# Exp on VectorE in eight steps with integer bits, in three of four head groups of every block

## The chip, the cores and the metric

The kernel runs on one core of a Trainium2 chip. The metric is the device time of one launch in microseconds. An execution with the hardware profiler gives the trace; times of other executions give the median.

Engines are called as in the profile: PE is TensorE (PEld its weight loads), ACT is ScalarE, DVE is VectorE, POOL is GpSimd, SP is SyncE, which issues most of the DMAs.

## The reference, cut to what matters

Four graph layers run one after the other on a node matrix x (3327 x 128) and an adjacency matrix adj (3327 x 3327). Each is followed by a residual addition and a layer normalisation. Only layer 0 is touched by the change. It is an attention with a transposed view of heads: 128 "heads" d, each with 3327 queries and keys of only 8 features, and adj added twice to the scores.

```python
q = (x @ Wq.T).reshape(d, n, h)          # d = 128, n = 3327, h = 8
k = (x @ Wk.T).reshape(d, n, h)
v = (x @ Wv.T).reshape(d, n, h)
a = jnp.einsum('dnh,dmh->dnm', q, k) * d ** (-0.5)
a = a + adj + adj
a = softmax(a, axis=2)
out = jnp.einsum('dnm,dmh->dnh', a, v).reshape(n, h * d)
return out @ Wo.T
```

So the exponential of 128 x 3327 x 3327 scores has to be taken, about 1.4 billion of them. The later layers multiply adj and its transpose with 128-column matrices.

## The kernel before, in words

**Stages.** The start (to about 319 us in the trace) projects x to queries, keys and values, splits queries and keys in a high and a low half and lays them down in DRAM scratch. The attention (`attention()`, lines 409 to 686) follows, to about 10141 us. The other layers take the rest, to 10914 us.

**Blocks.** The attention goes through 28 blocks: 7 chunks of 476 queries (`CW`), and for each 4 stretches of key tiles of 128 keys (`KBS`, line 80): 7, 7, 6 and 6 tiles. So 14 blocks have seven key tiles and 14 have six. In a block all 128 d are gone through, in 32 groups of four (`GROUP`). A block and a d make one step.

**A step.** Scores of one d are made in three sets of key tiles (`SETS`, line 444): 3, 2 and 2 tiles in a seven-tile block, 2, 2 and 2 in a six-tile block. Each set has its own PSUM buffer `sc` (line 421), one of each, so a set can be refilled only when the exponential of the same set of the step before has been read out. `exponents` (line 594) issues a set's score matmuls (L610) and then its exponential: as a rule one ACT activation (L618), which reads the whole set from PSUM and writes a tile `e` to SBUF with 476 columns per key tile. Only in the first d of a group, and only for the third set (`si` 2), in the groups that `on_vector` (line 446) names, does DVE take the exponential instead: `vector_exp` (line 568). In a seven-tile block these are groups 0, 1 and 2 of every four; in a six-tile block every even group. That is 24 exps in a seven-tile block and 16 in a six-tile block, 560 in all; the other 10192 sets go to ACT.

**Exp on DVE before.** L574 reads the scores from PSUM, clamps them and scales them by 2/ln 2. L575 rounds by adding a large constant, L576 takes the difference of rounded and unrounded value, L577 shifts the rounded number's bits into the exponent and sets mantissa bits, and five steps of L580 evaluate a polynomial; the last of them multiplies by the power of two. Nine instructions on 128 x 952 elements. The tiles `ey` and `et` that they share exist once each.

**Edges.** In the first step of a block (d = 0) adj is first turned into each PSUM buffer by PE transposes (L603), four per key tile; the scores are added onto it. The same PSUM contents serve every later d of the block, because the queries and keys of one d come with the negated ones of the d before: keys and queries have 32 more rows that subtract the previous d's scores. `copy_queries` (line 495) makes these negated copies on DVE, three instructions (L499, L500, L501) per group, one group ahead. `load_edges` (line 429) fetches the edges of the next block with two DMAs on SP's queue, right after the third set of d = 0.

**Weighing.** `weigh` (line 624) multiplies the finished exponentials of one key tile, for the four d of a group, with the values (four matmuls, L635; the trace counts eight). The weighings of a group, 7 or 6, are spread over the next group's twelve places (4 d x 3 sets) by the table `PLACES` (line 452): after the set at place p come as many weighings as the row has entries p. After every third group the sum in PSUM is added to `acc` by DVE (L646, L648).

**What orders the work.** The order on PE, ACT, POOL and DVE in the attention is the program's own (`manual_schedule`). The DVE steps behind the first of an exp, and the query copies, stand in a list `vec`; `vector_work` (line 585) takes from it as long as a running cost of DVE, `clock[1]`, is below that of the sets, `clock[0]` (0.95 per set in seven-tile, 0.84 in six-tile blocks). The first step, L574, is issued at its place. A weighing that needs a DVE exponential takes out of the list what belongs to its group first.

**Background pieces.** In the attention's first 24 blocks or so, the transpose of adj and its row and column sums are made in pieces, one piece in eight groups (`PACE`): load and store in groups 0 of eight, DVE transpose and maximum in group 3, DVE sums in group 7 (`background`, `background_work`, lines 526 and 533).

**Loads.** For every group, SP issues three DMAs of queries (L469) and eight of keys (L476), two groups ahead, and every second group one of values (L511).

Of the kernel before, what the change touches and what calls it, by code (L numbers as in the profile page):

```python
# [19 lines left out]
P = 128  # L20
# [7 lines left out]

POLY = (-7.287735661479654, 41.808648955824374, -180.93753376132258, 522.0867441991364, -753.2122427382569)
ROUND = 1.5 * 2 ** 23 + 127 + 256 - 10
MANTISSA = 3015794
EPS = 1e-5


# [14 lines left out]
def kernel(ctx: ExitStack, tc: tile.TileContext, x, adj, wq, wk, wv, wo,  # L51
# [357 lines left out]
    def attention():  # L409
        with tc.tile_pool(name="acc", bufs=1) as accp, tc.tile_pool(name="kq", bufs=3) as kq, \  # L410
# [15 lines left out]
            groups = [(b, g) for b in range(len(blocks)) for g in range(NHG)]  # L426
            steps = [(b, d) for b in range(len(blocks)) for d in range(D)]

            def load_edges(b):
                c0, kb = blocks[b]  # L430
                k0, nt = KBS[kb]
                w = min(nt * P, N - k0 * P)
                e = ed.tile([P, len(subs), 7 * P], F32, name="e_in")
                if w < nt * P:
                    nc.gpsimd.memset(e[:, :, w:nt * P], 0.0)
                nf = CW // P
# [87 lines left out]
            loaded, worked, turning = [], [], []  # L524

            def background(n):
                if n % PACE == 0 and worked:
                    piece_store(pe, *worked.pop(0))
                if n % PACE == 0 and pieces:
                    u, c = pieces.pop(0)  # L530
                    loaded.append((u, c, piece_load(pe, u, c)))

            def background_work(n):
                if n % PACE == 3 and loaded:
                    u, c, ai = loaded.pop(0)
                    steps = piece_work(pe, u, c, ai)
                    worked.append((u, c, next(steps)))
                    next(steps)
                    clock[1] += 2.4
                    turning.append(steps)  # L540
                if n % PACE == 7 and turning:
                    clock[1] += 2.4
                    for _ in turning.pop():
                        pass

            def prepare(b, d):

# [12 lines left out]

                if d % GROUP == 1 - on_vector(KBS[blocks[b][1]][1], d // GROUP) and n + 1 < len(groups):
# [6 lines left out]
            def vector_exp(e, x, of):  # L568


                y = ex.tile([P, 2, CW], F32, name="ey")
                t = ex.tile([P, 2, CW], F32, name="et")
                ti = t.bitcast(I32)
                nc.vector.tensor_scalar(y, x, -58 * math.log(2.0), 2 / math.log(2.0), ALU.max, ALU.mult)  # L574
                vec.append((0.7, of, lambda: nc.vector.tensor_scalar(t, y, ROUND, None, ALU.add)))  # L575
                vec.append((1.2, of, lambda: nc.vector.scalar_tensor_tensor(y, t, ROUND, y, ALU.subtract, ALU.subtract)))  # L576
                vec.append((0.7, of, lambda: nc.vector.tensor_scalar(ti, ti, 23, MANTISSA, ALU.logical_shift_left,  # L577
                                                                 ALU.bitwise_or)))
# [15 lines left out]
            def exponents(b, d, si):  # L594
# [16 lines left out]
                                     rhs=qt[64 * rg:64 * rg + 64, k, :],  # L611
                                     start=False, stop=True, skip_group_check=True)
                e = ex.tile([P, (3, 2, 2)[si], CW], F32, tag=f"e{si}", name=f"e{si}", bufs=(6, 7, 8)[si])
                if on_vector(nt, d // GROUP) and (d % GROUP, si) == (0, 2):
                    vector_exp(e[:, 0:n, :], s[:, 0:n, 0:CW], (b, d // GROUP))
                    clock[1] += 1.2
                else:
                    nc.scalar.activation(e[:, 0:n, :], s[:, 0:n, 0:CW], AF.Exp, scale=2.0)  # L618
# [42 lines left out]
            queue, place = [], 0  # L661
            with tc.manual_schedule(engines={mybir.EngineType.PE, mybir.EngineType.Activation,
                                             mybir.EngineType.Pool, mybir.EngineType.DVE}):
                edges[0] = load_edges(0)
# [5 lines left out]
                for b, d in steps:  # L670
                    prepare(b, d)
                    for si in range(len(SETS[KBS[blocks[b][1]][1]])):
                        vector_work(b)
                        exponents(b, d, si)
                        for _ in range(PLACES[len(queue_of)][d // GROUP % 4].count(place) if queue else 0):
                            weigh(*queue.pop(0))
                        place += 1
                    if d % GROUP == GROUP - 1:
                        while queue:
                            weigh(*queue.pop(0))  # L680
                        queue_of = [(b, d // GROUP, r) for r in range(KBS[blocks[b][1]][1])]
                        queue, place = list(queue_of), 0
# [562 lines left out]
```

## Time and profile before

| | us |
|---|---|
| median of 3 runs | 10919.42 (10911.48 to 10927.48) |
| the profiled execution's own time | 10915.5 |
| its span, first to last instruction | 10913.7 |
| busy: PE, ACT, DVE, POOL | 10590.0, 9774.0, 8351.7, 1667.9 |
| a block of seven key tiles | 369.75 to 371.5 for most (first 390.75, one 382.5) |
| a block of six key tiles | about 328.75 |

The span is what the engines show; the time adds 1.8 us around it. In the lists of groups a line reads: source line, engine, operation, output <- input with shapes and types, count, then busy us and mean ns of one, then the engine's idle time just before and what ended it. In a timeline a line reads: start, duration, engine, line, operation, how many instructions are merged, and in brackets the idle time of that engine before it and what ended that. In a line of windows each engine's busy time stands with its count of instructions; then follow the granted TensorE clock, the busy share of the DMA engines and GB/s. The granted clock was 0.995 over the run.

### The profile page before, as it was taken

How to read it: one execution, taken by the hardware profiler on the slowest of the kernel's cores; microseconds unless marked ns; L12 is line 12 of the kernel's file. 1: busy time of each engine (PE TensorE's matmuls, PEld its weight loads, DVE VectorE, ACT ScalarE, POOL GpSimd, SP SyncE). 2: the span in 40 equal slices, each digit the busy share in tenths (PEclk: the TensorE clock that was granted, in tenths of full speed). 3: DMA queues.
4: the chain of work that ended last, by engine and by line, in shares of the span. 5: the costliest groups of instructions: out<-in, count | busy, mean ns of one | idle time of the engine just before them, and what ended most of it. 6: DMA issues, size and time to landing. Idle time of an engine off the chain costs nothing. (4 is left out here: it accounts for less than half of the span.)

```text
span 10913.7 us, 202710 instructions
## 1 busy us (share of the span) xinstructions
PE 10590.0 (97%) x76941; PEld 4114.5 (38%) x76941; DVE 8351.7 (77%) x9359; ACT 9774.0 (90%) x10671; POOL 1667.9 (15%) x2742
## 2 busy tenths in 40 slices
PE   8899999999999999999999999999999999999999
PEld 5333333333333333333333333333333333333779
DVE  6788778887788877788877888778887788777312
ACT  3799999999999999999999999999999999999400
POOL 0111122111221111211112111121111100001200
PEclk9899999999999999999999999999999999999999
DMA  7888888888888888888888888888888888788676
GB/s 252 155 127 123 129 133 133 128 124 127 136 133 128 124 127 131 136 123 127 131 131 135 115 122 121 123 133 129 126 129 123 120 119 117 116 111 118 209 283 245
DMA packets 995063, 1516.19 MB, mean 139 GB/s; under 512 B 202471, under 2 KB 812577, under 8 KB 980267
## 3 DMA queue, kind: packets, MB, share of 16 engines
q1 hardware_dynamic: 896854, 1371.75, 77.5%
q0 software_dynamic: 79616, 116.88, 4.7%
q8 instruction: 623, 10.21, 0.5%
q10 hardware_dynamic: 17620, 14.49, 0.4%
q14 instruction: 350, 2.87, 0.1%
HBM read 1371.86 MB, written 130.35 MB: 138 GB/s over the span
## 5 line engine op out<-in xcount | busy, mean ns | idle before, releaser
L618 ACT ACTIVATE e<-sc 128x952 f32<-128x952 f32 (+1 forms) x10192 | 9551.3, 1076 | 281.1 <-PE sc L610 274.7
L635 PE MATMUL o<-e,v_pad 128*32 128x476 f32 (+1 forms) x46592 | 5657.5, 573 | 47.1 <-DVE acc L648 39.8
L610 PE MATMUL sc<-qt,kt 64*128 64x476 f32 x23296 | 4503.2, 439 | 178.4 <-ACT e L618 113.1
L610 PEld LDWEIGHTS sc<-qt,kt 64*128 64x128 f32 x23296 | 2197.0, 184 | 4570.9 <-ACT e L618 4015.0
L580 DVE SCALAR_TENSOR_TENSOR e<-e,ey 128x952 f32<-128x952 f32 x1680 | 1932.7, 1150 | 52.3
L515 POOL COPY v_pad<-vs 128x192 f32<-128x192 f32 (+1 forms) x896 | 534.4, 622 | 7986.1 <-DMA vs<-v_img 5559.1
L635 PEld LDWEIGHTS o<-e,v_pad 128*32 128x32 f32 (+1 forms) x46592 | 1027.9, 108 | 1904.7 <-issue 1858.7
L574 DVE TENSOR_SCALAR ey<-sc 128x952 f32<-128x952 f32 x560 | 643.9, 1150 | 1047.2 <-PE sc L610 1041.2
L501 DVE CAST qt<-qt 64x1904 fp32r<-64x1904 f32 x896 | 1032.8, 1153 | 30.4
L499 DVE TENSOR_SCALAR qt<-qt 32x1428 fp32r<-32x1428 f32 x896 | 807.6, 901 | 159.2 <-DMA qt<-q_s 100.6
L234 POOL DMA_DIRECT2D adjT_s<-at x1352 | 785.3, 587 | 234.5 <-DMA adjT_s<-at 162.2
L580 DVE SCALAR_TENSOR_TENSOR e<-e,et 128x952 f32<-128x952 f32 x560 | 647.5, 1156 | 17.8
L576 DVE SCALAR_TENSOR_TENSOR ey<-et,ey 128x952 f32<-128x952 f32 x560 | 645.1, 1152 | 19.4
L580 DVE SCALAR_TENSOR_TENSOR e<-ey 128x952 f32<-128x952 f32 x560 | 642.0, 1146 | 0.0
L1081 PE MATMUL bank<-y,eT 128*128 128x128 f32 (+1 forms) x4056 | 473.9, 276 | 0.4 <-DVE h L1203 0.4
L1081 PEld LDWEIGHTS bank<-y,eT 128*128 128x128 f32 (+1 forms) x4056 | 465.3, 192 | 5.7 <-DVE h L1203 0.6
L648 DVE TENSOR_TENSOR acc<-o,acc 128x476 f32<-128x476 f32 x231 | 150.3, 651 | 312.4 <-PE o L635 312.0
L575 DVE TENSOR_SCALAR et<-ey 128x952 f32<-128x952 f32 x560 | 372.6, 665 | 18.7
L577 DVE TENSOR_SCALAR et<-et 128x952 int32<-128x952 int32 x560 | 371.1, 663 | 19.3
L500 DVE TENSOR_SCALAR qt<-qt 32x476 fp32r<-32x476 f32 x896 | 360.2, 402 | 7.8 <-DMA qt<-lead_s 3.5
L1041 ACT ACTIVATE rstd<-mv,eps 128x1 f32<-128x1 f32 x104 | 30.4, 293 | 265.5 <-DVE mv L1039 265.5
L655 POOL DMA_DIRECT2D o_s<-acc x308 | 191.4, 625 | 34.9 <-DVE acc L648 22.0
(152 smaller groups left out, 2402.6 us busy)
## 6 DMA issues: line engine op xcount, KB each, us to landing
kt<-k_s SPq DMA_DIRECT2D x5320, 96.0 KB
kt<-k_s SPq DMA_DIRECT2D x1764, 128.0 KB
eT<-adjT_s SPq DMA_DIRECT2D x78, 1664.0 KB
qt<-q_s SPq DMA_DIRECT2D x896, 119.0 KB
qt<-q_s SPq DMA_DIRECT2D x1792, 59.5 KB
vs<-v_img SPq DMA_DIRECT2D x224, 224.0 KB
adjT_s<-at POOLq DMA_DIRECT2D x1352, 32.0 KB, 6.0
vs<-v_img SPq DMA_DIRECT2D x224, 192.0 KB
```

The costliest lines, as they stand in the source:

```text
L234: nc.gpsimd.dma_start(out=flat_ap(adjT_s, (t * P + 32 * q) * NP + c * PIECE, [[NP, 32], [P, ns], [1, P]]), in_=at[32 * i:32 * i + 32].rear ...
L499: return [(0.9, None, lambda: nc.vector.tensor_scalar(qt[32:64, 1:], qf[0:32, 0:GROUP - 1], -1.0, None, ALU.mult)), (0.4, None, lambda: nc ...
L501: (1.2, None, lambda: nc.vector.tensor_copy(qt[64:128], qf[0:64]))]
L515: nc.gpsimd.tensor_copy(vp[:, 32:32 + nt * GROUP * 32].rearrange("p (x c) -> p x c", c=32)[:, :, 0:H], vs.rearrange("p (x c) -> p x c", c=H))
L574: nc.vector.tensor_scalar(y, x, -58 * math.log(2.0), 2 / math.log(2.0), ALU.max, ALU.mult)
L575: vec.append((0.7, of, lambda: nc.vector.tensor_scalar(t, y, ROUND, None, ALU.add)))
L576: vec.append((1.2, of, lambda: nc.vector.scalar_tensor_tensor(y, t, ROUND, y, ALU.subtract, ALU.subtract)))
L580: vec.append((1.2, of, lambda i=i, a=a: nc.vector.scalar_tensor_tensor(e, e if i else y, a, t if i == len(POLY) - 1 else y, ALU.add, ALU.m ...
L610: nc.tensor.matmul(s[:, i, 0:CW], lhsT=kt[64 * rg:64 * rg + 64, k, pos * P:(pos + 1) * P], rhs=qt[64 * rg:64 * rg + 64, k, :], start=False ...
L618: nc.scalar.activation(e[:, 0:n, :], s[:, 0:n, 0:CW], AF.Exp, scale=2.0)
L635: nc.tensor.matmul(o[32 * j:32 * j + 32, 0:CW], lhsT=values[b, g][:m, c:c + 32], rhs=es[b, g * GROUP + j, r][:m, :], start=(r == 0 and u = ...
L1081: nc.tensor.matmul(ps[:n, 0:D], lhsT=e[:m, s, :n], rhs=y[:m, s, col:col + D], start=(s == 0), stop=(s == T - 1))
```

## The change

- **Exp in eight steps.** The first step writes a whole number (int32): the clamped score times 2^24/ln 2. One step takes its upper bits and makes the power of two of them by a bitwise AND and XOR; one takes its lower 23 bits and makes a float between 0.25 and 0.5 of them by AND and OR. Five steps of the polynomial follow, with new coefficients. The step that took the difference (L576) is gone.
- **Which groups.** `on_vector` no longer asks for the kind of block: groups 1, 2 and 3 of every four in all blocks. That is 24 x 28 = 672 exps on DVE and 10080 sets on ACT.
- **Places.** `PLACES` has other rows; the six-tile row is the same for all groups, (0, 2, 4, 6, 8, 10). A new table `FIRST` holds the places in the first group of a block: none before place 4.
- **Edges in four loads.** Each of the four query parts has its own DMA, issued after the third set of d = 0, 8, 16 and 24.
- **Background.** Load and store move to groups 2 of eight, transpose and maximum to groups 4, sums to groups 0.

```diff
-POLY = (-7.287735661479654, 41.808648955824374, -180.93753376132258, 522.0867441991364, -753.2122427382569)
-ROUND = 1.5 * 2 ** 23 + 127 + 256 - 10
-MANTISSA = 3015794
+POLY = (-0.12145248055458069, 1.287218689918518, 0.8447736501693726, 0.7106341123580933, 0.24892811477184296)
+UPPER, LOWER = 0x7F800000, 0x7FFFFF
+EXPONENT, QUARTER = 0x40000000, 0x3E800000
...
-            def load_edges(b):
+            def load_edges(b, j):
...
+                if j == 0:
+                    edges[b] = ed.tile([P, len(subs), 7 * P], F32, name="e_in")
...
-                nc.sync.dma_start(out=e[:, 0:nf, 0:w],
-                                  in_=flat_ap(adj, c0 * N + k0 * P, [[N, P], [P * N, nf], [1, w]]))
-                nc.sync.dma_start(out=e[0:CW - nf * P, nf, 0:w],
-                                  in_=flat_ap(adj, c0 * N + (nf * P * N + k0 * P), [[N, CW - nf * P], [1, w]]))
-                return e
+                q0, n = subs[j]
+                nc.sync.dma_start(out=edges[b][0:n, j, 0:w],
+                                  in_=flat_ap(adj, (c0 + q0) * N + k0 * P, [[N, n], [1, w]]))
...
-            def on_vector(nt, g):
-                return g % 4 != 3 if nt == 7 else g % 2 == 0
+            def on_vector(g):
+                return g % 4 != 0
...
-            PLACES = {7: ((0, 0, 4, 7, 7, 10, 10), (0, 0, 4, 7, 7, 9, 10), (1, 1, 4, 6, 8, 10, 10),
-                          (0, 2, 3, 5, 7, 8, 10)),
-                      6: ((0, 0, 3, 6, 8, 10), (0, 2, 4, 5, 7, 9)) * 2}
+            PLACES = {7: ((0, 2, 4, 4, 7, 7, 9), (0, 0, 3, 7, 7, 10, 10), (0, 0, 3, 6, 6, 9, 9), (0, 0, 3, 6, 7, 10, 10)),
+                      6: ((0, 2, 4, 6, 8, 10),) * 4}
+
+            FIRST = {7: (4, 4, 5, 7, 7, 10, 10), 6: (4, 4, 7, 7, 10, 10)}
...
-                if n % PACE == 0 and worked:
+                if n % PACE == 2 and worked:
...
-                if n % PACE == 0 and pieces:
+                if n % PACE == 2 and pieces:
...
-                if n % PACE == 3 and loaded:
+                if n % PACE == 4 and loaded:
...
-                if n % PACE == 7 and turning:
+                if n % PACE == 0 and turning:
...
-                ti = t.bitcast(I32)
-                nc.vector.tensor_scalar(y, x, -58 * math.log(2.0), 2 / math.log(2.0), ALU.max, ALU.mult)
-                vec.append((0.7, of, lambda: nc.vector.tensor_scalar(t, y, ROUND, None, ALU.add)))
-                vec.append((1.2, of, lambda: nc.vector.scalar_tensor_tensor(y, t, ROUND, y, ALU.subtract, ALU.subtract)))
-                vec.append((0.7, of, lambda: nc.vector.tensor_scalar(ti, ti, 23, MANTISSA, ALU.logical_shift_left,
+                yi, ti = y.bitcast(I32), t.bitcast(I32)
+                nc.vector.tensor_scalar(yi, x, -58 * math.log(2.0), 2 ** 24 / math.log(2.0), ALU.max, ALU.mult)
+                vec.append((0.7, of, lambda: nc.vector.tensor_scalar(ti, yi, UPPER, EXPONENT, ALU.bitwise_and,
+                                                                 ALU.bitwise_xor)))
+                vec.append((0.7, of, lambda: nc.vector.tensor_scalar(yi, yi, LOWER, QUARTER, ALU.bitwise_and,
                                                                  ALU.bitwise_or)))
...
-                if on_vector(nt, d // GROUP) and (d % GROUP, si) == (0, 2):
+                if on_vector(d // GROUP) and (d % GROUP, si) == (0, 2):
...
-                if d == 0 and si == len(SETS[nt]) - 1 and b + 1 < len(blocks):
-                    edges[b + 1] = load_edges(b + 1)
+                if d % (2 * GROUP) == 0 and d // (2 * GROUP) < len(subs) and si == len(SETS[nt]) - 1 \
+                        and b + 1 < len(blocks):
+                    load_edges(b + 1, d // (2 * GROUP))
...
-                        for _ in range(PLACES[len(queue_of)][d // GROUP % 4].count(place) if queue else 0):
-                            weigh(*queue.pop(0))
+                        if queue:
+                            at = PLACES[len(queue_of)][d // GROUP % 4] if d >= GROUP else FIRST[len(queue_of)]
+                            for _ in range(at.count(place)):
+                                weigh(*queue.pop(0))
```

More of the change, by code (lines that the diff above doesn't have):

```diff
@@ L432, in load_edges @@
                 w = min(nt * P, N - k0 * P)
[L433 to L436, printed above, removed]
-                nc.sync.dma_start(out=e[:, 0:nf, 0:w],
-                                  in_=flat_ap(adj, c0 * N + k0 * P, [[N, P], [P * N, nf], [1, w]]))
-                nc.sync.dma_start(out=e[0:CW - nf * P, nf, 0:w],
-                                  in_=flat_ap(adj, c0 * N + (nf * P * N + k0 * P), [[N, CW - nf * P], [1, w]]))
-                return e
-            SETS = {7: [(0, 3), (3, 2), (5, 2)], 6: [(0, 2), (2, 2), (4, 2)]}
-            def on_vector(nt, g):
-                return g % 4 != 3 if nt == 7 else g % 2 == 0
-            PLACES = {7: ((0, 0, 4, 7, 7, 10, 10), (0, 0, 4, 7, 7, 9, 10), (1, 1, 4, 6, 8, 10, 10),
-                          (0, 2, 3, 5, 7, 8, 10)),
-                      6: ((0, 0, 3, 6, 8, 10), (0, 2, 4, 5, 7, 9)) * 2}
+                if j == 0:
+                    edges[b] = ed.tile([P, len(subs), 7 * P], F32, name="e_in")
+                    if w < nt * P:
+                        nc.gpsimd.memset(edges[b][:, :, w:nt * P], 0.0)
+                q0, n = subs[j]
+                nc.sync.dma_start(out=edges[b][0:n, j, 0:w],
+                                  in_=flat_ap(adj, (c0 + q0) * N + k0 * P, [[N, n], [1, w]]))
+            SETS = {7: [(0, 3), (3, 2), (5, 2)], 6: [(0, 2), (2, 2), (4, 2)]}
+            def on_vector(g):
[3 more added lines that the diff above has]
+            FIRST = {7: (4, 4, 5, 7, 7, 10, 10), 6: (4, 4, 7, 7, 10, 10)}
             def load_heads(b, g):
@@ L558, in prepare @@
                     background(n)
-                if d % GROUP == 1 - on_vector(KBS[blocks[b][1]][1], d // GROUP) and n + 1 < len(groups):
+                if d % GROUP == 1 - on_vector(d // GROUP) and n + 1 < len(groups):
                     vec.extend(copy_queries(*groups[n + 1]))
@@ L663, in attention @@
                                              mybir.EngineType.Pool, mybir.EngineType.DVE}):
-                edges[0] = load_edges(0)
+                for j in range(len(subs)):
+                    load_edges(0, j)
                 for n in range(2):
```

## The prediction, made before the changed kernel had been run

> **What bounds the kernel now.** I read the page, then the windows of single blocks, the groups by form, and the timeline inside a block and across a block's start.
>
> ```profile
> PE 10590.0 (97%) x76941; PEld 4114.5 (38%) x76941; DVE 8351.7 (77%) x9359; ACT 9774.0 (90%) x10671; POOL 1667.9 (15%) x2742
> ...
> 2107.75:2477.50 369.75, 363.45 (x2718) 128.98 (x2716) 325.94 (x344) 362.26 (x361) 60.50 (x97) 1.00 0.84 126
> 2477.50:2806.25 328.75, 320.98 (x2338) 106.83 (x2336) 251.19 (x277) 319.71 (x370) 59.69 (x106) 1.00 0.82 128
> ```
>
> The second and third lines are one block of seven key tiles and one of six (columns: us, then busy of PE, PEld, DVE, ACT, POOL). The attention's 28 blocks, 14 of each kind, run from 319 to about 10141 us. ACT is busy 97 to 98% in both, DVE 88% and 76%.
>
> ```profile
> L618 ACT ACTIVATE e<-sc 128x952 f32<-128x952 f32 x8400 | 7532.5, 1006 | 209.5 <-PE sc L610 203.2
> L618 ACT ACTIVATE e<-sc 128x1428 f32<-128x1428 f32 x1792 | 2518.2, 1405 | 71.6 <-PE sc L610 71.5
> L574 DVE TENSOR_SCALAR ey<-sc 128x952 f32<-128x952 f32 x560 | 643.9, 1150 | 1047.2 <-PE sc L610 1041.2
> L577 DVE TENSOR_SCALAR et<-et 128x952 int32<-128x952 int32 x560 | 371.1, 663 | 19.3
> L576 DVE SCALAR_TENSOR_TENSOR ey<-et,ey 128x952 f32<-128x952 f32 x560 | 645.1, 1152 | 19.4
> ```
>
> DVE does 560 exps of a set of two tiles in nine steps, ACT the rest. The third line's idle time is DVE waiting for scores: it has time left.
>
> ```profile
> 2585.34 19.88 ACT L618 ACTIVATE e<-sc 128x952 f32<-128x952 f32 x23 [0.34 <-PE sc L610]
> 2597.19 0.48 PE L610 MATMUL sc<-qt,kt 64*128 64x476 f32 x2
> 2597.60 1.01 PE L635 MATMUL o<-e,v_pad 128*32 128x476 f32 x8
> 2598.54 0.70 PE L610 MATMUL sc<-qt,kt 64*128 64x476 f32 x4
> 2603.30 1.80 PE L635 MATMUL o<-e,v_pad 128*32 128x476 f32 x16
> 2605.03 0.91 PE L610 MATMUL sc<-qt,kt 64*128 64x476 f32 x6
> 2605.55 0.97 ACT L618 ACTIVATE e<-sc 128x952 f32<-128x952 f32 x1 [0.33 <-PE sc L610]
> ```
>
> A six-tile block repeats every two groups: 23 activations end to end, then a gap. From run to run is 20.21 us. The run less its last instruction (about 0.98) gives 18.90/22 = **0.86 us per activation**, so the gap costs 20.21 - 23 x 0.86 = 0.43. It comes from PE: two weighings (x16) stand between sets 0 and 1. PE's rules from these lines: a weighing (x8) starts 0.42 after a set, the next set 0.94 after it; a second weighing adds 0.80; sets follow each other by 0.21; ACT starts 0.52 after a set's first matmul; and a buffer is free about 0.98 after ACT starts. So ACT is the bound, and PE's order costs it small gaps.
>
> ```profile
> 2482.32 0.97 ACT L618 ACTIVATE e<-sc 128x952 f32<-128x952 f32 x1 [2.07 <-PE sc L610]
> 2483.97 4.39 ACT L618 ACTIVATE e<-sc 128x952 f32<-128x952 f32 x5 [0.69 <-PE sc L610]
> ...
> 2113.06 0.97 ACT L618 ACTIVATE e<-sc 128x952 f32<-128x952 f32 x1 [1.70 <-PE sc L610]
> 2114.93 10.26 ACT L618 ACTIVATE e<-sc 128x1428 f32<-128x1428 f32 x10 [0.91 <-PE sc L610]
> ```
>
> At a block's start ACT stands 3.1 us (six tiles) or 3.75 us (seven): PE turns the edges in and does two weighings between them.
>
> **What the Trainium skill says.** "VectorE: DVE Perf Modes", the perf-mode tier table: fp32 tensor_scalar from SBUF runs at 2x, from PSUM or with two tensors at 1x. The trace agrees: 663 ns at L577 against 1150. "DVE: scalar operands, raw-bit mode, write accounting and state across instructions", Raw-bit mode: AND, OR and XOR pass raw 32-bit lanes; it gives no speed. L577, int32 with two such operations in place, took 663. "ScalarE: Activation LUTs", What ACT_TABLE_LOAD costs: 0.833 ns per element, neighbours overlapping by about 93 ns. The trace has (1405 - 1006)/476 = 0.838, and an overlap of 1.006 - 0.86 = 0.146, so the 0.86 is what one activation is worth. "Perfetto Trace Analysis", Identifying the Most-Contended Engine: matmul occupancy is no measure of the bound. The trace agrees: PE reads 97%, while two sets and a weighing need 1.57 us against ACT's 1.72.
>
> **The change part by part.**
>
> *Exp in eight steps.* Gone are L576 (1.15) and L575's float add; in come two bit operations, priced as L577 (0.66). The first step now writes int32. No row shows that from PSUM; I take 1.15, with bounds 1.10 and 1.50. The bit operations lie between 0.65 and 1.15 (1x). One exp: 1.15 + 2 x 0.66 + 5 x 1.15 = 8.22 busy against 9.37; with start-to-start spacing (1.18 and 0.67 in the timeline) 8.40. DVE isn't the bound, so this alone gives nothing: it makes room.
>
> *Three of four groups everywhere.* Seven-tile blocks keep 24 exps on DVE; only the group left out moves. Six-tile blocks go from 16 to 24: 8 x 14 = 112 activations leave ACT, 112 x 0.86 = 96 us. DVE there gets 24 x 8.22 - 16 x 9.37 = +47 busy, 251 to 298 of some 322 (93%).
>
> *Rounds, six tiles.* Now a weighing stands after every second set, also right behind DVE's set 2. Put ACT's start on set 0 at 0. PE starts set 0 at -1.61, the weighing at -1.19, set 1 at -0.25, DVE's set at 0.12 (its buffer's release), the weighing at 0.54, the next set 0 at 1.48, ready at 2.00. ACT wants it at 1.72: gap 0.28. The sets after it come in time. The same rules give 0.38 for the old gap, measured 0.43, so I take 0.34. Four groups: before 2 x 20.21 = 40.42; after 45 x 0.86 + 3 x 0.34 = 39.72; **-0.70**, times 8 x 14 = **-78**. Of the 0.86 of the activation saved, 0.16 goes to three gaps in place of two. Queued behind the weighing that makes the gap is the next set 0, and ACT waits for that.
>
> *Does DVE keep up?* Its copies for the next group (0.82 + 0.42 + 1.18) stand ahead of or around the first step. First step in group 1 at 0.72, exp done 9.12, two copies 10.36; group 2's set is ready at 10.5; exp and third copy done 20.1, a copy and in a third of groups a flush (0.67), so group 3's first step starts at 21.0 to 21.6, 0.6 to 1.3 late. Its buffer is wanted again 1.3 after the first step could have begun. It just fits, and group 0, without exp, clears the debt. Price if it doesn't: every 0.1 late is 11 us.
>
> *The first group.* No weighing stands among the turned sets and ACT does all three. Six tiles, from the lines above: set 1 ready at 2480.6 where 2480.1 is wanted, set 2 0.5 late: 1.0 instead of 2.9. But six weighings then go in pairs into nine sets: 3 x 0.21 + 0.21 + 0.94 + 0.80 = 2.58, no slack against 3 x 0.86, and such pairs leave gaps of 0.17 now. I take -1.3 of a possible -2 to 0. Seven tiles: set 1 0.1 late, set 2 0.5, with the first 0.5: 1.1 instead of 3.1; the longer set 0 gives the pairs slack: -1.9 (-2.5 to 0). **14 x 3.2 = -45.**
>
> *Seven tiles, steady.* Two gaps of about 0.22 per four groups now; the new places keep double weighings at place 0. Zero, between -0.2 and +0.35 per four groups (-22 to +39).
>
> *Edges in four loads*, issued at steps 0, 8, 16 and 24: 54 more DMAs net on SP's queue (27 blocks), each ahead of one group's queries and keys. Needed 100 steps later. Zero; before, the one burst made the next keys' issue last 10 us without stopping ACT, so small gains are more likely than losses. Background pieces move by two or one groups of eight; transposes fall into group 0, which has no exp: zero, their cover being group 0's idle DVE, otherwise 2.4 us each late.
>
> **Sum:** -78 - 45 = -123. The profiled execution took 10915.5 (span 10913.7); the median, 10919.4, is 0.04% above it. 10919.4 - 123 = **10796**.
>
> **Rivals.** (1) *DVE half late*: group 3's first step misses by 0.5 more than my chain has, for 93% load says so; 0.5 x 112 = 56 back: 10852. Against it: group 0 resets the debt. (2) *Slower*: the int32 first step at 1.50 and both bit operations at 1.15, an exp of 9.7. Then group 3's first step is 3.2 late, 1.9 past what its buffer allows, at PE's next set 2: 1.9 - 0.7 = 1.2 x 112 = +134, less 45: 11008. It turns slower when an exp takes about 0.8 us more than 8.4. Against it: L577 at 663. (3) *No effect*: places and loads give back what 112 activations bring, within 0.2%, about what this measurement can tell from no change: 10915. Only the sum of three upper bounds gets there. (4) *More*: the gap behind DVE's set vanishes and the starts give 4: 10750.
>
> **Chances:** forecast 0.70 (10765 to 10830 its own), (1) 0.14, (2) 0.07, (3) 0.04, (4) 0.05. The range 10760 to 10880 holds the first two. Faster 0.89, same 0.04, slower 0.07.
>
> **What would show it.** Six-tile blocks of 321 to 323 us with 360 activations, a gap near 0.3 in each DVE group, L574 near 1150 and the bit steps near 663; starts with 1 to 2 us of idle ACT; seven-tile blocks of 367 to 369. Wrong, if PE waits long for L574, if six-tile blocks stay above 326, or if the bit steps take 1150.

## The result, and the profile after

| | before | after |
|---|---|---|
| median, us | 10923.45 of 4 runs (10911.48 to 10932.62) | 10792.15 of 4 runs (10790.81 to 10797.75) |
| profiled span, us | 10913.7 | 10791.2 |
| blocks of seven key tiles, median us | 370.1 | 368.7 and 367.9, by turns |
| blocks of six key tiles, mean us | 328.8 | 322.2 |

The ratio of the times is 0.9881, 95% interval 0.9864 to 0.9899. The change made the kernel 131 us faster; 10796 was forecast; the profiled spans, which are of one execution each, differ by 122.5. A block's length is taken here from the first turned edge of one block to that of the next. Over the blocks, six tiles give 13 x 6.6 = 86 us of the 122.5 (the end of the last of them has no next edge), seven tiles (14 of them) 31.

The page's line of busy times, and the windows of one block of each kind (us, then busy PE, PEld, DVE, ACT, POOL with their counts), of the kernel after:

```profile
PE 10545.2 (98%) x76941; PEld 4103.4 (38%) x76941; DVE 8700.0 (81%) x9695; ACT 9680.6 (90%) x10559; POOL 1852.8 (17%) x2742
...
2087.00:2455.50 368.50, 361.38 (x2718) 129.46 (x2716) 302.07 (x321) 363.59 (x361) 61.54 (x97) 1.00 0.84 127
2455.50:2778.00 322.50, 320.02 (x2338) 105.23 (x2336) 297.55 (x322) 311.65 (x361) 67.14 (x105) 1.00 0.87 131
```

ACT is busy 97 to 99% of both blocks, as before: it still bounds them. In the six-tile block DVE went from 251 to 298 us, 92% of it, and in the seven-tile block from 326 to 302, since an exp is shorter there and their number is the same. PE reads 98%, but did the same matmuls before in a longer time; its share says nothing of the bound.

The groups by form show what the exp costs now:

```profile
L574 DVE TENSOR_SCALAR ey<-sc 128x952 int32<-128x952 f32 x672 | 772.1, 1149 | 624.6 <-PE sc L610 615.1
...
L577 DVE TENSOR_SCALAR ey<-ey 128x952 int32<-128x952 int32 x672 | 447.1, 665 | 23.3
L575 DVE TENSOR_SCALAR et<-ey 128x952 int32<-128x952 int32 x672 | 443.1, 659 | 22.5
```

The first step, which now writes int32 from PSUM, takes 1149 ns (1150 as fp32 before), and the bit operations 659 and 665 ns. All eight together are 1.149 + 0.659 + 0.665 + 5 x 1.151 = 8.23 us, against 8.22 forecast. "VectorE: DVE Perf Modes" of the Trainium skill, the perf-mode tier table, gives 2x to fp32 tensor_scalar from SBUF; the bit operations on int32 run at the same rate.

ACT's timeline in the six-tile block:

```profile
2512.28 9.53 ACT L618 ACTIVATE e<-sc 128x952 f32<-128x952 f32 x11 [0.30 <-PE sc L610]
2522.12 9.53 ACT L618 ACTIVATE e<-sc 128x952 f32<-128x952 f32 x11 [0.31 <-PE sc L610]
2531.95 19.81 ACT L618 ACTIVATE e<-sc 128x952 f32<-128x952 f32 x23 [0.30 <-PE sc L610]
2552.06 9.53 ACT L618 ACTIVATE e<-sc 128x952 f32<-128x952 f32 x11 [0.30 <-PE sc L610]
```

Four groups now are runs of 11, 11 and 23 activations, 45 in all, and take 2552.06 - 2512.28 = 39.78 us (forecast 39.72, 40.42 in the stretch of before that the prediction took). At 0.86 us per activation 45 of them are 38.70, so each of the three gaps costs 0.36 (forecast 0.34).

All engines around the second and third of these gaps:

```profile
2521.84 1.15 DVE L574 TENSOR_SCALAR ey<-sc 128x952 int32<-128x952 f32 x1
...
2529.80 1.15 DVE L580 SCALAR_TENSOR_TENSOR e<-e,et 128x952 f32<-128x952 f32 x1
...
2529.80 0.70 PE L610 MATMUL sc<-qt,kt 64*128 64x476 f32 x4
2530.43 1.00 PE L636 MATMUL o<-e,v_pad 128*32 128x476 f32 x8
2530.86 1.14 DVE L574 TENSOR_SCALAR ey<-sc 128x952 int32<-128x952 f32 x1
2531.37 0.81 PE L610 MATMUL sc<-qt,kt 64*128 64x476 f32 x4
2531.95 2.67 ACT L618 ACTIVATE e<-sc 128x952 f32<-128x952 f32 x3 [0.30 <-PE sc L610]
```

The weighing (L636) stands behind DVE's set and ahead of the next set 0, which starts 0.94 us after it; ACT waits for that set. This is the gap, in the place where the rules had it. On DVE, one exp's first step at 2530.86 follows directly on the last step of the exp before it: no slack is left there. That it still is in time shows in PE's waits:

```profile
PE sc L610 <- DVE ey L574: 18.1, 34, 2.2
```

PE waited 18 us in all of the 10791 for DVE's first step (24.3 before). Its weight loads waited another 153 us for it (163 before).

The starts of a six-tile and of a seven-tile block on ACT:

```profile
2781.08 0.97 ACT L618 ACTIVATE e<-sc 128x952 f32<-128x952 f32 x1 [0.34 <-PE sc L610]
2782.46 10.82 ACT L618 ACTIVATE e<-sc 128x952 f32<-128x952 f32 x12 [0.42 <-PE sc L610]
2793.95 6.96 ACT L618 ACTIVATE e<-sc 128x952 f32<-128x952 f32 x8 [0.66 <-PE sc L610]
...
2089.32 2.29 ACT L618 ACTIVATE e<-sc 128x1428 f32<-128x1428 f32 x2 [0.96 <-PE sc L610]
2092.03 3.93 ACT L618 ACTIVATE e<-sc 128x952 f32<-128x952 f32 x4 [0.42 <-PE sc L610]
2096.43 7.49 ACT L618 ACTIVATE e<-sc 128x1428 f32<-128x1428 f32 x7 [0.47 <-PE sc L610]
```

The gaps of 2.07 and 1.70 us that the prediction shows are gone, but the pairs of weighings leave one of 0.66 later. ACT's idle time in the first 20 us of a block, taken from the timeline for all blocks but the first, has a mean of 3.8 before and 1.7 after with seven tiles, and of 3.15 and 2.1 with six.

### The profile page after: what moved, and what is told of

It reads as the page before. It is cut to its first block, busy times and chain, and to the rows that moved or that the text cites. A ratio compares the mean times of both kernels' runs of the same rounds, so it can differ in the third digit from the quotient of the medians.

```text
span 10791.2 us, 203132 instructions
## 1 busy us (share of the span) xinstructions
PE 10545.2 (98%) x76941; PEld 4103.4 (38%) x76941; DVE 8700.0 (81%) x9695; ACT 9680.6 (90%) x10559; POOL 1852.8 (17%) x2742
## 5 line engine op out<-in xcount | busy, mean ns | idle before, releaser
L636 PE MATMUL o<-e,v_pad 128*32 128x476 f32 (+1 forms) x46592 | 5621.3, 573 | 38.2 <-DVE acc L649 25.5
L580 DVE SCALAR_TENSOR_TENSOR e<-e,ey 128x952 f32<-128x952 f32 x2016 | 2319.7, 1151 | 66.4
L515 POOL COPY v_pad<-vs 128x192 f32<-128x192 f32 (+1 forms) x896 | 606.7, 702 | 7666.8 <-DMA vs<-v_img 5875.9
L636 PEld LDWEIGHTS o<-e,v_pad 128*32 128x32 f32 (+1 forms) x46592 | 1045.1, 108 | 1967.2 <-issue 1931.9
L574 DVE TENSOR_SCALAR ey<-sc 128x952 int32<-128x952 f32 x672 | 772.1, 1149 | 624.6 <-PE sc L610 615.1
L234 POOL DMA_DIRECT2D adjT_s<-at x1352 | 853.5, 638 | 232.6 <-DMA adjT_s<-at 168.2
L580 DVE SCALAR_TENSOR_TENSOR e<-ey 128x952 f32<-128x952 f32 x672 | 773.5, 1151 | 23.3
L580 DVE SCALAR_TENSOR_TENSOR e<-e,et 128x952 f32<-128x952 f32 x672 | 774.1, 1152 | 20.7
L577 DVE TENSOR_SCALAR ey<-ey 128x952 int32<-128x952 int32 x672 | 447.1, 665 | 23.3
L575 DVE TENSOR_SCALAR et<-ey 128x952 int32<-128x952 int32 x672 | 443.1, 659 | 22.5
L647 DVE COPY acc<-o 128x476 f32<-128x476 f32 x77 | 50.1, 650 | 136.4 <-PE o L636 135.8
```

Of the source, the lines that this page charges most:

```text
L234: nc.gpsimd.dma_start(out=flat_ap(adjT_s, (t * P + 32 * q) * NP + c * PIECE, [[NP, 32], [P, ns], [1, P]]), in_=at[32 * i:32 * i + 32].rear ...
L515: nc.gpsimd.tensor_copy(vp[:, 32:32 + nt * GROUP * 32].rearrange("p (x c) -> p x c", c=32)[:, :, 0:H], vs.rearrange("p (x c) -> p x c", c=H))
L574: nc.vector.tensor_scalar(yi, x, -58 * math.log(2.0), 2 ** 24 / math.log(2.0), ALU.max, ALU.mult)
L575: vec.append((0.7, of, lambda: nc.vector.tensor_scalar(ti, yi, UPPER, EXPONENT, ALU.bitwise_and, ALU.bitwise_xor)))
L577: vec.append((0.7, of, lambda: nc.vector.tensor_scalar(yi, yi, LOWER, QUARTER, ALU.bitwise_and, ALU.bitwise_or)))
L636: nc.tensor.matmul(o[32 * j:32 * j + 32, 0:CW], lhsT=values[b, g][:m, c:c + 32], rhs=es[b, g * GROUP + j, r][:m, :], start=(r == 0 and u = ...
```

## The experiments

**Theory**: ACT bounds the blocks; the time comes from 112 activations that leave it, under places that allow it, and from the starts; DVE's exp in eight steps only makes the room, with group 0 as its reserve. **Rivals**: the shorter exp itself is worth something, or the places alone are, or the edge loads; or DVE has more room than the theory says, so that nine steps or other groups would do as well. "Before" and "after" stand for the two kernels.

Each kernel was timed beside the kernel before (medians between 10913.18 and 10917.71). Kernels built on after are compared with after at 10792.15, or at its second measurement:

> The changed kernel once more, beside the kernel before on this chip, as the base of the differences of all experiments: 10792 by the first measurement, 10783 if its ratio of 0.988 holds against 10914.

It took **10789.09** (10787.06 to 10794.81), ratio 0.9883 [0.9868, 0.9898]. The medians of after thus differ by 3 us, and those of before by 10 (10913.18 to 10923.45), so a difference of a few us between two kernels means nothing.

### Two of four groups in six-tile blocks

```diff
-            def on_vector(g):
+            def on_vector(nt, g):
...
-                return g % 4 != 0
+                return g % 4 != 0 if nt == 7 else g % 2 == 1
```

> The changed kernel, but in six-tile blocks only groups 1 and 3 of four have their exp on VectorE: 112 exps go back to ScalarE. My theory: one activation more (0.86) and one gap of 0.37 less per four groups, 0.49 x 112 = 55: 10847 (10835 to 10865), six-tile blocks 3.9 us longer, seven-tile blocks unchanged. Rival (the gain comes from places, edges and first group): 10792, within 12.

It took **10822.39** (10818.48 to 10825.58), ratio 0.9916 [0.9899, 0.9932]: 30 to 33 us more than after, where 55 was expected. ACT's timeline in a six-tile block:

```profile
2883.65 19.81 ACT L618 ACTIVATE e<-sc 128x952 f32<-128x952 f32 x23 [0.30 <-PE sc L610]
2903.75 19.81 ACT L618 ACTIVATE e<-sc 128x952 f32<-128x952 f32 x23 [0.29 <-PE sc L610]
2923.86 19.81 ACT L618 ACTIVATE e<-sc 128x952 f32<-128x952 f32 x23 [0.30 <-PE sc L610]
```

Four groups take 2923.86 - 2883.65 = 40.21 us. Call four groups a stretch. A block has eight; the first and the last are under the influence of the edges, so the middle six of the 14 six-tile blocks are taken, 84 stretches. Their mean length is 40.70 us before, 40.22 here and 39.93 after. The 40.42 from which the prediction starts is the shorter of two kinds: before, 28 of the 84 take 40.46 us, and the other 56 take 40.82; in these PE waits 0.1 us or more for the flush of the weighings into `acc`, as here:

```profile
2613.69 1.00 PE L635 MATMUL o<-e,v_pad 128*32 128x476 f32 x8 [0.40 <-DVE acc L648]
```

So of the 0.77 by which a middle stretch got shorter, 0.48 comes without the third exp. Half of that, 0.24, is the flush waits, which no middle stretch has here; the other 0.24 goes with the new places, under which the same 46 activations leave 0.66 us for two gaps instead of 0.90. The third exp nets 0.29, and 0.29 x 112 = 32 us is what this kernel is slower by. In an undisturbed stretch of after it is worth 40.21 - 39.78 = 0.43, which would be 48 us in all. The other 16 are lost where three exps leave DVE late: in a block's first and last stretch, around background pieces, and also in the six-tile blocks after the last piece, where every third stretch takes 40.1 to 40.3 us. An instance in the block shown above, PE's wait and then ACT's gap:

```profile
2643.44 0.70 PE L610 MATMUL sc<-qt,kt 64*128 64x476 f32 x4 [0.74 <-DVE ey L574]
...
2643.97 7.82 ACT L618 ACTIVATE e<-sc 128x952 f32<-128x952 f32 x9 [0.62 <-PE sc L610]
```

DVE's first step stood there behind a piece's last small steps and three query copies.

### The old places for six tiles

```diff
-                      6: ((0, 2, 4, 6, 8, 10),) * 4}
+                      6: ((0, 0, 3, 6, 8, 10), (0, 2, 4, 5, 7, 9)) * 2}
```

> The changed kernel with the old rows of places in six-tile blocks (first group as changed). My theory: worked out with the same PE rules, the old rows leave gaps of about 0.4 and 0.8 us in turn instead of 0.3 in each group with an exp and 0.4 in a group without: 1.5 us per four groups more, 1.5 x 112 = 168: 10960 (10900 to 11000), slower than before. Rival (ScalarE's count alone decides): 10792, within 15.

It took **10935.43** (10931.80 to 10940.98), ratio 1.0019 [1.0011, 1.0028]: slower than before, with 112 activations less. One period of four groups:

```profile
2876.28 10.46 ACT L618 ACTIVATE e<-sc 128x952 f32<-128x952 f32 x12 [0.33 <-PE sc L610]
2887.04 2.68 ACT L618 ACTIVATE e<-sc 128x952 f32<-128x952 f32 x3 [0.30 <-PE sc L610]
2890.08 6.10 ACT L618 ACTIVATE e<-sc 128x952 f32<-128x952 f32 x7 [0.36 <-PE sc L610]
2896.51 11.24 ACT L618 ACTIVATE e<-sc 128x952 f32<-128x952 f32 x13 [0.33 <-PE sc L610]
2908.22 2.67 ACT L618 ACTIVATE e<-sc 128x952 f32<-128x952 f32 x3 [0.47 <-PE sc L610]
2911.16 6.10 ACT L618 ACTIVATE e<-sc 128x952 f32<-128x952 f32 x7 [0.26 <-PE sc L610]
2917.59 3.60 ACT L618 ACTIVATE e<-sc 128x952 f32<-128x952 f32 x4 [0.34 <-PE sc L610]
```

The 45 activations are there, but with six gaps instead of three: 2917.59 - 2876.28 = 41.31 us. The middle stretches have a mean of 41.36, where before has 40.70. The activation saved is worth 0.86, and PE's order takes back 1.52: the new row is what lets the third exp pay.

### Nine steps

This kernel has the old constants and the old exp in three of four groups, and issues what is left of one exp before the next begins.

```diff
+                while any(o is not None for _, o, _ in vec):
+                    vec.pop(0)[2]()
...
-                nc.vector.tensor_scalar(yi, x, -58 * math.log(2.0), 2 ** 24 / math.log(2.0), ALU.max, ALU.mult)
...
+                nc.vector.tensor_scalar(y, x, -58 * math.log(2.0), 2 / math.log(2.0), ALU.max, ALU.mult)
+                vec.append((0.7, of, lambda: nc.vector.tensor_scalar(t, y, ROUND, None, ALU.add)))
+                vec.append((1.2, of, lambda: nc.vector.scalar_tensor_tensor(y, t, ROUND, y, ALU.subtract, ALU.subtract)))
+                vec.append((0.7, of, lambda: nc.vector.tensor_scalar(ti, ti, 23, MANTISSA, ALU.logical_shift_left,
...
```

> The changed kernel with the old nine-step exp (and what is left of an exp is issued before the next one begins). My theory (in six-tile blocks the eight steps only just fit): an exp of 9.55 us from start to start puts the third exp of every four groups 2.8 to 3.5 us late, 1.3 of that are free, so 1.5 to 2.2 us per four groups in 112 such stretches: 10792 + 170 to 245, i.e. 10960 to 11040, slower than before; seven-tile blocks unchanged within 1.5 us each, six-tile blocks at 334 to 339 us. Rival (DVE never limits, the gain is ScalarE's 112 activations whatever the exp takes): 10792, within 15.

It took **11000.50** (10993.32 to 11006.06), ratio 1.0079 [1.0062, 1.0096], 208 to 211 us more than after and inside what the theory gave. Its six-tile blocks have a mean of 335.7 us, as expected; its seven-tile blocks are 2 us longer, where at most 1.5 was expected. A wait of PE, and ACT's timeline in a six-tile block (L612, L620 and L576 are here the scores, ACT's exp and the first step):

```profile
PE sc L612 <- DVE ey L576: 199.5, 244, 2.1
```

```profile
2907.31 18.10 ACT L620 ACTIVATE e<-sc 128x952 f32<-128x952 f32 x21 [1.19 <-PE sc L612]
2925.71 9.73 ACT L620 ACTIVATE e<-sc 128x952 f32<-128x952 f32 x11 [0.30 <-PE sc L612]
2936.10 9.53 ACT L620 ACTIVATE e<-sc 128x952 f32<-128x952 f32 x11 [0.66 <-PE sc L612]
```

PE now waits 200 us for the first step, and what stands behind it in PE's order reaches ACT as gaps of 0.66 and 1.19. This is the mechanism of the prediction's slower rival, with an exp of 9.37 us in place of 8.23.

### Pieces' DVE work in groups that have an exp

```diff
-                if n % PACE == 4 and loaded:
+                if n % PACE == 5 and loaded:
...
-                if n % PACE == 0 and turning:
+                if n % PACE == 1 and turning:
...
+                while any(o is not None for _, o, _ in vec):
+                    vec.pop(0)[2]()
```

> The changed kernel with the background pieces' VectorE work moved from groups 4 and 0 of eight to groups 5 and 1, which carry an exp (and what is left of an exp is issued before the next one begins). My theory: groups without an exp are the only place where VectorE has 5 us to spare; 2.4 to 2.6 us in group 1 of four make the next two exps late by about 2.2 and 3, of which 1.3 is free: about 2 us each of some 90 times in six-tile blocks, up to 1 in seven-tile blocks: 10792 + 150 to 270, i.e. 10940 to 11060. Rival (VectorE has 7% left and the place doesn't matter): 10792, within 15.

It took **10903.11** (10899.78 to 10909.70), ratio 0.9991 [0.9984, 0.9998]: 111 to 114 us more than after, in the expected direction and below the expected 150 to 270. In six-tile blocks, in the mean 7.7 us longer than those of after, ACT waits behind DVE again:

```profile
PE sc L612 <- DVE ey L576: 126.3, 147, 3.3
```

```profile
2511.46 18.09 ACT L620 ACTIVATE e<-sc 128x952 f32<-128x952 f32 x21 [0.99 <-PE sc L612]
```

The two six-tile blocks after the last piece whose length can be taken are as long as in after (321.8 and 322.8 us against 321.8 and 322.9). So it is the pieces that cost the time, not the second edit, and group 0's idle DVE is their cover. Seven-tile blocks, with DVE less loaded, grew by only 0.9 us.

### The first group with an ordinary row

```diff
-                            at = PLACES[len(queue_of)][d // GROUP % 4] if d >= GROUP else FIRST[len(queue_of)]
+                            at = PLACES[len(queue_of)][d // GROUP % 4]
```

> The changed kernel without the table for a block's first group: the ordinary row for groups 0 is used there, so single weighings stand again between the turned sets. My theory: about 1.1 to 1.6 us more idle ScalarE at each block's start, 28 x 1.3 = 36: 10828 (10812 to 10850). Rival (idle time at the start is made up later or the pairs in the first group eat it): 10792, within 12.

It took **10807.88** (10806.89 to 10809.81), ratio 0.9902 [0.9886, 0.9919]: 16 to 19 us more than after, half of what was expected. The same two starts on ACT:

```profile
2784.74 0.96 ACT L618 ACTIVATE e<-sc 128x952 f32<-128x952 f32 x1 [1.27 <-PE sc L610]
2786.13 0.97 ACT L618 ACTIVATE e<-sc 128x952 f32<-128x952 f32 x1 [0.42 <-PE sc L610]
...
2092.99 0.96 ACT L618 ACTIVATE e<-sc 128x952 f32<-128x952 f32 x1 [0.90 <-PE sc L610]
```

Mean idle ACT in a block's first 20 us is 2.7 with seven tiles and 2.9 with six: between before (3.8, 3.15) and after (1.7, 2.1). So about half of what the starts gained in idle time comes from the rest of the change, not from `FIRST`. What part of the rest brings it was not separated; the new ordinary rows and a group 0 without an exp are candidates.

### Edges in two loads at once

```diff
-                q0, n = subs[j]
-                nc.sync.dma_start(out=edges[b][0:n, j, 0:w],
...
+                e, nf = edges[b], CW // P
+                nc.sync.dma_start(out=e[:, 0:nf, 0:w],
...
+                nc.sync.dma_start(out=e[0:CW - nf * P, nf, 0:w],
...
-                if d % (2 * GROUP) == 0 and d // (2 * GROUP) < len(subs) and si == len(SETS[nt]) - 1 \
+                if d == 0 and si == len(SETS[nt]) - 1 \
```

> The changed kernel with the next block's edges loaded as before, two DMAs after the third set of d = 0. My theory: the loads are needed 100 steps later and only delay keys that have two groups of time: 10792, within 12. Rival (the burst of 1.3 MB delays queries and keys of the next groups): 0.5 to 1.5 us per block, 10806 to 10834, with waits of ScalarE for sets in the second and third group of a block.

It took **10795.89** (10794.67 to 10800.71), ratio 0.9892 [0.9876, 0.9909]. No effect of the four loads is shown.

### The eight steps alone, on the kernel before

```diff
-                vec.append((1.2, of, lambda: nc.vector.scalar_tensor_tensor(y, t, ROUND, y, ALU.subtract, ALU.subtract)))
...
+                nc.vector.tensor_scalar(yi, x, -58 * math.log(2.0), 2 ** 24 / math.log(2.0), ALU.max, ALU.mult)
+                vec.append((0.7, of, lambda: nc.vector.tensor_scalar(ti, yi, UPPER, EXPONENT, ALU.bitwise_and,
...
+                vec.append((0.7, of, lambda: nc.vector.tensor_scalar(yi, yi, LOWER, QUARTER, ALU.bitwise_and,
...
```

> The kernel before with the eight-step exp alone; groups, places, edges and background as before. My theory (ACT sets the pace, DVE has room): 560 exps get 1.15 us shorter on DVE, and the time stays at 10923, within 15 us; L574's busy mean 1150 ns, the two bit steps 660 to 670. Rival (the shorter exp itself brings the gain, because PE waits for DVE to let go of the third set's buffer, 187 us of such waits in the trace before): 30 to 100 us faster, 10823 to 10893.

It took **10959.18** (10951.01 to 10966.24), ratio 1.0043 [1.0029, 1.0058]: 45 us slower than before, with DVE doing less. Neither theory had that. PE's waits for the flush of the weighings into `acc`, before and then here:

```profile
PE o L635 <- DVE acc L648: 39.8, 102, 0.8
...
PE o L635 <- DVE acc L646: 6.0, 20, 1.1
```

```profile
PE o L635 <- DVE acc L648: 66.3, 126, 1.3
PE o L635 <- DVE acc L646: 19.7, 42, 1.8
```

The sum goes from 46 to 86 us. The timeline of this kernel shows such a wait:

```profile
2197.96 1.15 DVE L580 SCALAR_TENSOR_TENSOR e<-e,et 128x952 f32<-128x952 f32 x1
...
2199.03 0.65 DVE L648 TENSOR_TENSOR acc<-o,acc 128x476 f32<-128x476 f32 x1
...
2199.82 1.01 PE L635 MATMUL o<-e,v_pad 128*32 128x476 f32 x8 [0.47 <-DVE acc L648]
```

The flush stands behind a whole exp in DVE's queue, and PE's next weighing waits for it. The shorter exp lowers the running cost of `vec`, so more steps are issued ahead of what follows: of the 308 flushes 1 stood right behind the last step of an exp before and 112 do here. The same shift puts all 560 first steps behind the query copies (before, 154 stood between them), so two causes were open.

### The eight steps in the old order

As the last kernel, with the second bit step counted at 1.9 in the running cost. That restores the old order in DVE's queue exactly, and changes no instruction.

```diff
-                vec.append((0.7, of, lambda: nc.vector.tensor_scalar(yi, yi, LOWER, QUARTER, ALU.bitwise_and,
+                vec.append((1.9, of, lambda: nc.vector.tensor_scalar(yi, yi, LOWER, QUARTER, ALU.bitwise_and,
```

> E1 (eight-step exp alone) with one number changed: the second bit step is charged 1.9 in the running cost of VectorE instead of 0.7, what the two old steps cost together. VectorE's queue then has the order of the kernel before, without L576: 195 of the 308 flushes between the steps of an exp (84 in E1) and 154 of the 560 first steps between the query copies (0 in E1). New theory (E1 is slower because the shorter costs changed the order of VectorE's queue, not because of the steps): 10914, within 12, or up to 15 faster. Rival (the steps themselves, or VectorE running ahead, cost time): 10945 to 10960, as E1.

It took **10884.67** (10881.08 to 10891.53), ratio 0.9970 [0.9959, 0.9982]: faster than before by about 33 us, more than the 15 expected at most, and than the last kernel by 74 (by their ratios to before, 80). What PE waits for flushes:

```profile
PE o L635 <- DVE acc L648: 2.5, 8, 0.8
```

So the order alone is worth 74 to 80 us, and 86, 46 and 2.5 us of waits for flushes go with 10959, about 10916 and 10885 us. The sums of waits for the first step do not decide on the other cause: PE's own are 19.2 us in the last kernel and 35.1 here, but 143 and 120 with those of its weight loads. The stretches decide. Middle stretches of six-tile blocks:

| | without a flush wait, mean us | with one, mean us |
|---|---|---|
| before | 28 stretches, 40.46 | 56, 40.82 |
| eight steps alone | 28, 40.46 | 56, 40.97 |
| eight steps, old order | 83, 40.46 | 1, 41.21 |

In none of these does PE itself wait for a first step. Where no flush wait stands, the three kernels are equally fast, so the flushes are the cause there. Seven-tile blocks show the same: the median stretch of the slower kernel is 46.18 us with a flush wait and 45.67 without, and 45.75 in the faster one, which has none. That these waits fall below those of before when the order is the same fits a flush that comes sooner because the exp ahead of it is shorter.

### The copies behind the first step

A second way to part the two causes: the eight steps, and the query copies put into `vec` in the second step of a group always.

```diff
-                if d % GROUP == 1 - on_vector(KBS[blocks[b][1]][1], d // GROUP) and n + 1 < len(groups):
+                if d % GROUP == 1 and n + 1 < len(groups):
```

> E1 with the query copies put into the list after the exp's first step instead of before it, so that no first step waits behind copies of its own group that wait for their DMA; the flushes stay as in E1 (84 between the steps, 111 right behind an exp). If the first steps behind the copies make E1 slow: about 10914 to 10925. If the flushes behind the exps do (PE's next weighing waits for a flush): 10945 to 10960, as E1.

It took **13644.51** (13627.36 to 13648.32), ratio 1.2492 [1.2475, 1.2509]. ACT's wait for scores, 274.7 us before, is:

```profile
ACT e L618 <- PE sc L610: 2812.0, 1885, 4.6
```

The copies come behind the exp now, and the next group's scores wait for them. It says nothing on the question, only that the copies have to stay ahead. The granted TensorE clock, 0.908, was also lower than the 0.994 before.

### More exps on DVE

In seven-tile blocks seven of eight groups, with their own places in the added one; the pieces' transposes move to the group that stays without an exp.

```diff
-                return g % 4 != 0
+                return g % (8 if nt == 7 else 4) != 0
...
-                if n % PACE == 4 and loaded:
+                if n % PACE == 0 and loaded:
...
+                            if d // GROUP % 8 == 4 and len(queue_of) == 7:
+                                at = (1, 1, 3, 6, 6, 9, 9)
```

> An attempt to go on: in seven-tile blocks seven of eight groups have their exp on VectorE (its share there was 82%), the background pieces' VectorE work goes together into groups 0 of eight, and the group added has places (1, 1, 3, 6, 6, 9, 9). My theory: 56 activations leave ScalarE, 48 us, of which PE's order gives back about a third: 10760 (10745 to 10785). Rival (VectorE gets late over seven exps in a row, or PE has no room): 10792 or up to 10830.

It took **10795.64** (10792.74 to 10798.56), ratio 0.9890 [0.9873, 0.9906]: nothing gained, where 10760 was expected. Seven-tile blocks became 1.1 us shorter; six-tile blocks, whose pieces now all fall into one group, grew by 1.6. A first kernel to mend that gave no time: instructions in it wait for each other in a circle. The next kernel leaves the pieces of six-tile blocks where after has them:

```diff
-                if n % PACE == 4 and loaded:
+                if loaded and (n % PACE == 0 or n % PACE == 4 and KBS[blocks[n // NHG][1]][1] == 6):
```

> E8 again, with the background pieces' VectorE work put together in groups 0 of eight for pieces loaded in seven-tile blocks alone; six-tile blocks as in the changed kernel, with the transposes in groups 4. My theory: E8 won 1.1 us in a seven-tile block and lost 1.5 in a six-tile block, where one group had all the pieces' work; without that loss 14 x 1.1 = 15 us below the changed kernel (10789): 10774 (10766 to 10784). Rival (the loss in the six-tile blocks comes from elsewhere): 10789 to 10797.

It took **10782.35** (10779.04 to 10786.45), ratio 0.9878 [0.9862, 0.9895]. That is 7 to 10 us below after and within the expected 10766 to 10784; but the intervals of the two ratios overlap, so that it beats after is not shown. Here 56 more activations left ACT (14 x 4), worth at most 48 us at 0.86; most of that is taken back. DVE is busy 85% of the span.

## Why the prediction was right, point by point

- **What bounds it**: right. ACT stays at 97 to 99% in the blocks, and its gaps stand where PE's order puts them.
- **Prices of the exp**: right, 8.23 us against 8.22; both ends of the bounds for int32 and bit operations were not needed. (The fp32 tensor_scalar from SBUF in the trace before is L575, 665 ns; L577, which the prediction names for it, is the int32 step.)
- **"This alone gives nothing"**: wrong, the step whose reason failed. Alone, the eight steps cost 45 us in the order that the running cost then gives, and bring 33 in the old one. "DVE isn't the bound" overlooked a second product of DVE: the flush, for which PE's next weighing waits, and which stands in DVE's queue behind the exp. In after these waits (shown below) are 25.5 + 7.3 = 33 us against 46 before. By the median lengths of the middle stretches with and without them, an estimate from the two traces, they cost 20 us before in six-tile blocks (56 x 0.36) and 4 in seven-tile blocks (25 x 0.14), after 1 and 11 (23 x 0.06, 45 x 0.25). So about 12 us of the gain in these stretches went by this way, for which the sum has nothing.

```profile
PE o L636 <- DVE acc L649: 25.5, 80, 1.1
...
PE o L636 <- DVE acc L647: 7.3, 27, 0.7
```

- **Three of four groups, -78**: right in size, partly by luck. Six-tile blocks gained 14 x 6.6 = 92 us, of which their starts are 15; 77 are left. But the 40.42 was read from a stretch without a flush wait, and "repeats every two groups" holds only there; the mean is 40.70. The 0.77 per middle stretch are 0.24 of flush waits, 0.24 that go with the places, and 0.29 of the third exp, for which the forecast's own numbers give 0.52 (46 x 0.86 + 2 x 0.34 = 40.24, less 39.72). A gain that was overlooked made up for one that came out smaller. With the old places the third exp would have been a loss.
- **First groups, -45**: the sum of starts fits: 14 x (3.8 - 1.7) + 14 x (3.15 - 2.1) = -44. The reason given, no weighing among the turned sets, is about half of it in idle time, and 16 to 19 us of the kernel's time.
- **Seven tiles steady, zero**: right in sum. These blocks gained 2.2 us, and their starts alone 2.1. Two things cancel: a middle stretch without a flush wait went from 45.76 to 45.60 us, but 45 of 84 have such a wait after, and 25 before.
- **Edges, background**: zero, right for both, and the named cover is the real one: without group 0's idle DVE the pieces cost over 110 us.
- **DVE just fits**: right. The nine-step exp, 1.14 us longer, ends slower than before, as the point given for the slower rival (0.8 us) says; the point itself was not measured. The first rival, DVE half late, is there in small: irregular gaps such as the 0.62 above, which take about 16 of the third exp's 48 us.

The places, the third exp and the flush waits act on the same gaps, so these shares hold for the order in which they were taken apart. The two terms that were summed landed, 77 and 44 us; what they were credited to was partly wrong. Left open: an order in which after's flushes come sooner, as in the eight-step kernel in the old order, was not tried; by the estimate above it could save about 12 us in the middle stretches.

## What to carry to other kernels

When a bounding engine is relieved, work out where its gaps fall in the order of the engine that feeds it: here the same activations taken away gave a loss with one row of places and a gain with another. An engine that is not the bound still hands over small results; look for what waits for each of them and what stands ahead of it in that engine's queue. Where costs in a list decide an order, changing a cost moves other instructions, so compare the orders before putting a step down at zero.

## What the runs showed that was not expected

- The order of one engine's queue, with the same instructions, was worth 74 us (10959 to 10885), through flushes of 0.65 us each.
- A wait of the same length need not cost the same. A flush wait of 0.40 us in a middle stretch of six-tile blocks made it 0.36 longer before, one of 0.39 made it 0.06 longer after.
- An int32 first step from PSUM costs what the fp32 one did (1149 against 1150 ns), and bitwise steps on int32 in SBUF run like the fp32 one there (659 and 665 ns for 952 columns, against 665 for L575 before).
- With one weighing after every second set, each set that DVE takes costs ACT a gap of about 0.33 to 0.36 us, whether two or three of four groups have one.
